# Layer 0 of a two-layer graph network: the heads' product placed two node blocks later, the joined words in two copies, and the source scores of 13 row blocks transposed together

## The chip, the cores and the metric

The kernel runs on one core of one Trainium2 chip. The metric is the time of one execution on the device, in microseconds. The core has five engines with queues of their own: PE (matrix products, with PEld for its weight loads), DVE (vector), ACT (scalar), POOL and SP. The last two mostly issue transfers here. The transfers run on 16 DMA engines.

## The reference

There are 3327 nodes with 1024 features each. Layer 0 normalises the rows, quantises them, multiplies them by a quantised weight and by the weighted adjacency matrix, and adds the result to the input. Layer 1 normalises again, projects to 8 attention heads of 64, attends over the neighbours, and sends the result through four dense layers.

```python
# layer 0
h = jnp.maximum(_layernorm(x, axis=-1), 0.0)
x = x + _L0_gnn_ref(h, adj, ...)        # relu(xq @ wq), quantised; then adj @ support_q
# layer 1
h = jnp.maximum(_layernorm(x, axis=-1), 0.0)
...
Wh = jnp.einsum('nf,hfd->hnd', x, W)
e_src = jnp.einsum('hnd,hd->hn', Wh, a1)
e_dst = jnp.einsum('hnd,hd->hn', Wh, a2)
e = jax.nn.leaky_relu(e_src[:, :, None] + e_dst[:, None, :], ALPHA)
e = jnp.where(adj[None] > 0, e, NEG)
att = jax.nn.softmax(e, axis=-1)
h = jnp.einsum('hnm,hmd->hnd', att, Wh)
...
```

## The kernel before

Nodes are cut into T = 26 blocks of 128. A first stage quantises and makes the support `s_int` (26 tiles of 128 x 1024 that stay on the chip). It ends at about 125 us in the profile.

The second stage is the one that is changed. Its loop runs over 26 row blocks t of the output. For each of them the PE sums over 26 node blocks j the product of the adjacency (split into `hi` and `lo`, two fp32r parts) with `s_int[j]`: four products of 512 columns per j (two parts, two column halves), 104 per row block (L680). The j are taken in four groups, `PARTS`, of 7, 6, 7 and 6. `adjacency` loads a group on SP (`at`, L170, three buffers), casts it on ACT (`hi`, L174, two buffers), subtracts on DVE (`lo`, L178, two buffers), and writes the mask (`mk`, L179). It is called one group ahead.

After the 104 products of block t, ACT takes the sum out of PSUM (`y`, L695), DVE scales it (L696), adds the input (`xt`, L697, two buffers, loaded on SP at L128), POOL issues the store of that sum (`x1_d`, printed `x_d` in the profile, L698), and DVE makes the statistics of the layer norm and the normalised rows (L143 to L150). Then the rows are transposed for the heads (`transposed_by_dma`): ACT splits the 32-bit words into two 16-bit halves (`yh`, L587), SP issues a transposing DMA (`yht`, L589), and ACT joins the halves again (`ht`, L591). The last block is transposed by the PE instead.

`heads(t)` projects the rows: eight products of 512 columns (`whm`, L614; each shows twice in the profile, x16 for a block), a copy with the row's scale on ACT (`wht`, L620), two weighted sums on DVE (`src` and `dst`, L627 and L628), exponentials on ACT, a small PE transposition of `src` from 128 x 8 to 8 x 128 (`sp`, L633), its copy (`srct`, L635) and its store (`src_d`, L638, on POOL). Then come the features `ft`, `fw`, `dw` and their stores (`feat_d` L658, `dsum_d` L662, on POOL). The heads of block t run one row block later, in front of the last group of j of block t + 1:

```python
                    if js is PARTS[-1] and before is not None:
                        heads(*before)
                    for q, j in enumerate(js):
```

The order of instructions on each engine is fixed when the kernel is built, by a planner that follows estimated times, except for the instructions that `keep_in_program_order` pins. Each engine and each issuing queue works in that order.

The third stage, layer 1's attention, reads the stored features and source scores back (`f_even`, `f_odd`, `dw`, `srow`, on SP), makes the selection `sel` on DVE (L984) and multiplies on the PE (L993, L786). Its first products run between the last blocks of the second stage. The fourth stage is the dense layers.

Of the kernel before, what the change touches and what calls it, by code (L numbers as in the profile page):

```python
# [8 lines left out]
F32 = mybir.dt.float32  # L9
# [11 lines left out]
P = 128  # L21
N = 3327
T = (N + P - 1) // P
# [3 lines left out]
KF = F // P  # L27
FC = F // 512
NH = 8
# [13 lines left out]

SUBS = [range(0, 7), range(7, 13), range(13, 20), range(20, 26)]
PARTS = SUBS
GT = 2


# [12 lines left out]
def two_layer_kernel(  # L61
# [23 lines left out]
    nc = tc.nc  # L85

    const = ctx.enter_context(tc.tile_pool(name="const", bufs=1))
    dram = ctx.enter_context(tc.tile_pool(name="dram", bufs=1, space=DRAM))
    small = ctx.enter_context(tc.tile_pool(name="small", bufs=4))

    ident = const.tile([P, P], F32, name="ident")
    make_identity(nc, ident)
    ident_b = const.tile([P, P], BF16, name="ident_b")
    nc.vector.tensor_copy(ident_b, ident)
    ones = const.tile([P, P], F32, name="ones")
    nc.gpsimd.memset(ones, 1.0)
    nth = const.tile([P, P], F32, name="nth")
    nc.gpsimd.memset(nth, 1.0 / P)


    x1_d = dram.tile([NP, F], F32, name="x1_d")
# [3 lines left out]
    src_d = [dram.tile([NH, len(sub) * P], F32, name=f"src_d{i}") for i, sub in enumerate(SUBS)]  # L105
    enc_d = dram.tile([2, NP, EMB], U16, name="enc_d")

    const.tile([P, 32], F32, name="gap")
    ndst = const.tile([P, T, NH], F32, name="ndst")
    ratio = const.tile([P, T, NH], F32, name="ratio")  # L110


# [40 lines left out]
    def halves_of_words(words):  # L153

        return words.bitcast(U16).rearrange("p (n two) -> p two n", two=2)
# [7 lines left out]
    with tc.tile_pool(name="at", bufs=2, reuse_waits="tile") as atp:  # L163
# [35 lines left out]
        with tc.tile_pool(name="s1", bufs=2, reuse_waits="tile") as s1, tc.tile_pool(  # L199
            name="s1_mm", bufs=3, space=PSUM, reuse_waits="tile"  # L200
        ) as mm_ps, tc.tile_pool(name="s1_tp", bufs=2, space=PSUM, reuse_waits="tile") as tp_ps:
            w_int = s1.tile([P, KF, F], BF16, name="w_int", bufs=1)
            w_stats = s1.tile([P, 2 + 4 * (KF - 2), 3], F32, name="w_stats", bufs=1)

# [338 lines left out]
            for t in range(8, T):  # L543
                if t == T - 2:
                    part = next(columns)
# [26 lines left out]
        with tc.tile_pool(name="wh", bufs=1, reuse_waits="tile") as whp, tc.tile_pool(  # L572
            name="s2", bufs=2, reuse_waits="tile"
        ) as s2, tc.tile_pool(name="mm", bufs=2, space=PSUM, reuse_waits="tile") as mm_ps, tc.tile_pool(
            name="s2_wh", bufs=2, space=PSUM, reuse_waits="tile"
# [8 lines left out]
            def transposed_by_dma(y):  # L584

                yh = s2.tile([P, 2, F], U16, name="yh", bufs=1)
                nc.scalar.copy(yh, halves_of_words(y))  # L587
                yht = s2.tile([P, 2 * KF, P], U16, name="yht", bufs=1)
                nc.sync.dma_start_transpose(yht, yh.rearrange("p two f -> p (two f)"))  # L589
                ht = s2.tile([P, KF, P], F32, name="ht", bufs=1)  # L590
                nc.scalar.copy(  # L591
                    halves_of_words(ht.rearrange("p k i -> p (k i)")),
                    yht.rearrange("p (two k) i -> p two (k i)", two=2),
                )
                return ht

            def transposed_by_tensor(y):
# [9 lines left out]
            def heads(t, ht, r):  # L607
                if t == T - 1:
                    whm, sp = (last_ps.tile([P, EMB], F32, tag="last", name=n) for n in ("whm", "sp"))
                else:  # L610
                    whm = wh_ps.tile([P, EMB], F32, name="whm")
                    sp = sp_ps.tile([P, EMB], F32, name="sp")
                for k in range(KF):
                    ins = nc.tensor.matmul(  # L614
                        whm, ht[:, k, :], whead[:, k, :], start=(k == 0), stop=(k == KF - 1)
                    )
                    if k == 0 and t < T - 1:
                        tc.keep_in_program_order(ins)
                wht = s2.tile([P, EMB], F32, name="wht", bufs=1)
                ins = nc.scalar.activation(wht, whm, AF.Copy, scale=r)  # L620
                if t < T - 1:
                    tc.keep_in_program_order(ins)
                src = small.tile([P, NH], F32, name="src")
                dst = small.tile([P, NH], F32, name="dst")
                for a_t, e in ((a1_t, src), (a2_t, dst)):
                    prod = s2.tile([P, EMB], F32, name="prod", bufs=1)
                    nc.vector.tensor_tensor(prod, wht, a_t, ALU.mult)  # L627
                    nc.vector.tensor_reduce(  # L628
                        e, prod.rearrange("p (h d) -> p h d", d=HD), AX.X, ALU.add
                    )  # L630
                nc.vector.tensor_scalar(ndst[:, t], dst, -1.0, None, ALU.mult)
                nc.scalar.activation(ratio[:, t], src, AF.Exp, scale=1.0 - SLOPE)
                nc.tensor.transpose(sp[:NH, :P], src, ident)  # L633
                srct = s2.tile([NH, P], F32, name="srct")
                nc.scalar.copy(srct, sp[:NH, :P])  # L635
                for sub, d in zip(SUBS, src_d):
                    if t in sub:
                        nc.gpsimd.dma_start(d[:, (t - sub[0]) * P : (t - sub[0] + 1) * P], srct)  # L638

                ft = s2.tile([P, NH, 2, HC], F32, name="ft", bufs=1)  # L640
                wh3 = wht.rearrange("p (h d) -> p h d", d=HD)
                for q, slope in enumerate((1.0, SLOPE)):
                    nc.scalar.activation(ft[:, :, q, HD], dst, AF.Exp, scale=slope)
                    nc.vector.tensor_tensor(
                        ft[:, :, q, :HD], wh3, ft[:, :, q, HD:].to_broadcast([P, NH, HD]), ALU.mult
                    )
                fw = s2.tile([P, NH, 2, 2 * HC], F32R, name="fw", bufs=1)
                f2 = ft.rearrange("p h q c -> p h (q c)")
                nc.scalar.copy(fw[:, :, 0], f2)
                nc.vector.tensor_tensor(fw[:, :, 1], f2, fw[:, :, 0].bitcast(F32), ALU.subtract)  # L650

                dw = s2.tile([P, NPAIR, 2, 2, HC], F32R, name="dw", bufs=1)
                for q in range(2):
                    nc.scalar.copy(
                        dw[:, :, q],
                        fw[:, :, q, HC:].bitcast(F32).rearrange("p (g e) c -> p g e c", e=2),
                    )
                nc.gpsimd.dma_start(  # L658
                    feat_d[t].rearrange("h p c -> p h c"),
                    fw.bitcast(F32).rearrange("p h q c -> p h (q c)"),  # L660
                )
                nc.gpsimd.dma_start(  # L662
                    dsum_d[t].rearrange("g p c -> p g c"),
                    dw.bitcast(F32).rearrange("p g q e c -> p g (q e c)"),
                )

            before = None
            for t in range(T):
                xt = s2.tile([P, F], F32, name="xt2")
                load_rows(xt, x, t)  # L670
                mm = mm_ps.tile([P, F], F32, tag="mm", name="mm2")
                for js in PARTS:
                    hi, lo = part
                    part = next(columns, None)
                    if js is PARTS[-1] and before is not None:
                        heads(*before)
                    for q, j in enumerate(js):
                        for which in (hi, lo):
                            for c in range(FC):
                                nc.tensor.matmul(  # L680
                                    mm[:, c * 512 : (c + 1) * 512],
                                    which[:, q, :],
                                    s_int[j][:, c * 512 : (c + 1) * 512],
                                    start=(j == 0 and which is hi),
                                    stop=(j == T - 1 and which is lo),
                                )
                if t == 0:
                    for dst, ap in (
                        (whead, w_heads.rearrange("(k p) e -> p k e", p=P)),
                        (a1_t, a1.partition_broadcast(P)),  # L690
                        (a2_t, a2.partition_broadcast(P)),
                    ):
                        tc.keep_in_program_order(nc.sync.dma_start(dst, ap))
                y = s2.tile([P, F], F32, name="y", bufs=1)
                nc.scalar.activation(y, mm, AF.Copy, scale=r_asf)  # L695
                nc.vector.tensor_scalar(y, y, asf_t, sup_delta, ALU.mult, ALU.mult)  # L696
                nc.vector.tensor_tensor(xt, xt, y, ALU.add)  # L697
                nc.gpsimd.dma_start(x1_d[t * P : (t + 1) * P, :], xt)  # L698
                ln, r = normalised(y, xt)
                before = t, (transposed_by_tensor if t == T - 1 else transposed_by_dma)(y), r  # L700
# [419 lines left out]
```

## Time and profile before

| what | value |
|---|---|
| median of 3 runs | 2240.1 us (2240.02 to 2240.91) |
| profiled execution | 2241.67 us, span 2239.9 us |
| granted PE clock | 0.998 |
| layer 0's second stage | from about 125 to 936 us of the span |
| PE wait for `ht` | 7.0 us, 7 times, longest 1.4 |
| small transposition L633 | 26 times, 7.1 us busy, 273 ns each |
| copy `ht`, L591 | 25 times, 2.51 us each |
| transposing DMA `yht` | 25 times, 5.5 us from issue to landing (median) |
| store of `src_d` | 26 times, 4 KB, 1.6 us from issue to landing (median) |

The profile is one execution. Its times are in us from the first instruction. A line of the timeline gives start, duration, engine, line of the kernel, operation, what is written and what is read, the shapes, how many instructions were merged, and in brackets the idle time of the engine before it and what ended it. A group's line has busy time, mean ns of one and idle time. The PE's ends are modelled, so differences between starts are the safer measure there.

### The profile page before, as it was taken

To read this page: it belongs to the slowest core of one execution; us is meant where nothing else is said; L and a number is where in the kernel's file an instruction comes from. 1 tells how busy PE (TensorE), PEld (TensorE's weight loads), DVE (VectorE), ACT (ScalarE), POOL (GpSimd) and SP (SyncE) were. 2 spreads that over 40 slices of the span, in tenths; PEclk is the share of its full clock that TensorE was granted. 3 is DMA by queue.
4 is the path that set the end of the run, shared out by engine and by line. 5 is a ranking of instruction groups with operands and counts; after the bars stand their busy time and mean duration, and the time that the engine had idled before them with its cause. 6 is when DMAs were issued, how large, how long until landed. Compare 5 with 4: busy or idle time off the path is not lost.

```text
span 2239.9 us, 31268 instructions
## 1 busy us (share of the span) xinstructions
PE 2190.0 (98%) x12470; PEld 1747.2 (78%) x12480; DVE 1536.8 (69%) x1996; ACT 1114.9 (50%) x1685; POOL 180.4 (8%) x269
## 2 busy tenths in 40 slices
PE   5999999999999999899999999999999999999998
PEld 2477777766677777699999999999999999744444
DVE  8745555554455545588999999999999999822211
ACT  6734444444454444357566556565555655531120
POOL 2301101110111101000000000000000000000000
PEclk9999999999999999999999999999999999999999
DMA  6665566555665556934242341654242432383311
GB/s 216 161 196 158 157 182 183 170 168 146 183 181 171 162 158 189 310 128 148 83 139 88 93 131 33 225 175 151 86 148 83 138 89 77 100 208 104 113 56 56
DMA packets 241203, 321.68 MB, mean 144 GB/s; under 512 B 104021, under 2 KB 184869, under 8 KB 241057
## 3 DMA queue, kind: packets, MB, share of 16 engines
q1 hardware_dynamic: 220504, 246.50, 36.8%
q0 software_dynamic: 20544, 73.18, 10.4%
q8 instruction: 98, 1.61, 0.3%
q14 instruction: 49, 0.39, 0.1%
q10 hardware_dynamic: 8, 0.00, 0.0%
HBM read 209.25 MB, written 86.79 MB: 132 GB/s over the span
## 4 chain that ended last, share of the span: by engine, by line
PE 53%; ACT 1%; DVE 0%; DMA 0%; issue 0%; DVEq 0%
PE acc L993 27%; PE mps L786 13%; PE o L1064 8%; PE h_ps L1027 4%; ACT enct L1049 0%; PE h_ps L949 0%; DMA weights<-in_w1t 0%; ACT h L1034 0%; DVE sel L984 0%; DVE nodes L1060 0%; ACT su L830 0%; DVE su L827 0%; DVE yo L1074 0%; ACT rest L957 0%; DVEq L1117 0%
## 5 line engine op out<-in xcount | busy, mean ns | idle before, releaser
L984 DVE SCALAR_TENSOR_TENSOR sel<-srow,ndst,mask 128x896 fp32r<-128x896 f32 (+1 forms) x832 | 864.8, 1081 | 52.3 <-PE acc L993 47.2
L786 PE MATMUL mps<-dw,mf 128*128 128x260 f32 x2704 | 452.4, 283 | 0.1
L680 PE MATMUL mm<-s_int,hi 128*128 128x512 f32 x1352 | 427.2, 397 | 0.0
L680 PE MATMUL mm<-s_int,lo 128*128 128x512 f32 x1352 | 419.1, 391 | 0.0
L993 PE MATMUL acc<-f_even,sel 128*128 128x260 f32 x2704 | 399.6, 285 | 6.7 <-issue 5.0
L993 PE MATMUL acc<-f_odd,sel 128*128 128x260 f32 x2704 | 393.8, 286 | 1.0 <-ACT xs L1008 1.0
L785 ACT CAST mf<-mask 128x1664 fp32r<-128x1664 uint8 x208 | 331.4, 1594 | 113.0 <-PE mps L786 94.9
L786 PEld LDWEIGHTS mps<-dw,mf 128*128 128x128 f32 x2704 | 377.2, 188 | 0.5 <-ACT part L790 0.3
L993 PEld LDWEIGHTS acc<-f_even,sel 128*128 128x128 f32 x2704 | 356.8, 189 | 11.7 <-issue 5.9
L993 PEld LDWEIGHTS acc<-f_odd,sel 128*128 128x128 f32 x2704 | 352.5, 188 | 8.4 <-issue 3.4
L680 PEld LDWEIGHTS mm<-s_int,hi 128*128 128x128 f32 x1352 | 253.9, 188 | 63.6 <-issue 12.0
L680 PEld LDWEIGHTS mm<-s_int,lo 128*128 128x128 f32 x1352 | 252.0, 188 | 51.4
L179 DVE TENSOR_SCALAR mk<-at 128x896 uint8<-128x896 f32 (+1 forms) x104 | 62.0, 598 | 227.1 <-DMA at<-in_adj_t 226.8
L614 PE MATMUL whm<-whead,ht 128*128 128x512 f32 x416 | 184.4, 596 | 7.2 <-ACT ht L591 7.0
L1064 PE MATMUL o<-weights,h 128*128 128x512 f32 x416 | 179.9, 592 | 0.0
L1064 PEld LDWEIGHTS o<-weights,h 128*128 128x128 f32 x416 | 79.0, 190 | 99.3 <-issue 98.3
L614 PEld LDWEIGHTS whm<-whead,ht 128*128 128x128 f32 x416 | 77.6, 190 | 101.0 <-issue 87.1
L174 ACT CAST hi<-at 128x896 fp32r<-128x896 f32 x104 | 92.4, 889 | 125.6 <-PE mm L680 85.2
L790 ACT COPY part<-mps 128x260 f32<-128x260 f32 x104 | 39.3, 378 | 193.8 <-PE mps L786 193.8
L178 DVE TENSOR_TENSOR lo<-at,hi 128x896 fp32r<-128x896 f32 x104 | 106.0, 1020 | 42.8 <-ACT hi L174 42.6
L855 POOL DMA_DIRECT2D enc_d<-eh x64 | 57.5, 903 | 935.6 <-ACT eh L853 876.0
L1034 ACT ACTIVATE h<-h_ps,rest 128x512 f32<-128x512 f32 (+1 forms) x54 | 35.1, 653 | 195.0 <-PE h_ps L1027 195.0
(162 smaller groups left out, 1676.9 us busy)
## 6 DMA issues: line engine op xcount, KB each, us to landing
feat_d<-fw POOLq DMA_DIRECT2D x26, 1040.0 KB, 5.4
f_even<-feat_d SPq DMA_DIRECT2D x7, 3380.0 KB, 13.3
f_odd<-feat_d SPq DMA_DIRECT2D x7, 3380.0 KB, 13.2
at<-in_adj_t SPq DMA_DIRECT2D x52, 448.0 KB, 3.8
at<-in_adj_t SPq DMA_DIRECT2D x52, 384.0 KB, 3.2
mask<-mask_d SPq DMA_DIRECT2D x39, 416.0 KB, 6.5
dw<-dsum_d SPq DMA_DIRECT2D x16, 910.0 KB, 8.9
dsum_d<-dw POOLq DMA_DIRECT2D x26, 520.0 KB, 6.4
```

Source lines behind the costliest of these rows:

```text
L174: ins = nc.scalar.copy(hi, at)
L178: nc.vector.tensor_tensor(lo, at, hi.bitcast(F32), ALU.subtract)
L179: ins = nc.vector.tensor_scalar(mk[:, r], at, 0.0, None, ALU.is_gt)
L614: ins = nc.tensor.matmul(whm, ht[:, k, :], whead[:, k, :], start=(k == 0), stop=(k == KF - 1))
L680: nc.tensor.matmul(mm[:, c * 512 : (c + 1) * 512], which[:, q, :], s_int[j][:, c * 512 : (c + 1) * 512], start=(j == 0 and which is hi), s ...
L785: nc.scalar.copy(mf, mask[:, j : j + TH, :])
L786: nc.tensor.matmul(ps, mf[:, j % TH, :], dw[:, j, :], start=(j == 0), stop=(j == T - 1))
L855: nc.gpsimd.dma_start(enc_d[q, sub[0] * P : (sub[-1] + 1) * P, h * HD : (h + 1) * HD].rearrange("(b p) d -> p b d", p=P), eh[:, q].rearran ...
L984: nc.vector.scalar_tensor_tensor(sel[:, :nb], srow[:, :nb], ndst[:, j, h : h + 1], mask[:, :, j, :], ALU.is_gt, ALU.mult,)
L993: nc.tensor.matmul(accs[b], sel[:, b, :], f[:, j, :], start=(j == 0), stop=(j == T - 1))
L1027: nc.tensor.matmul(ps[:, :cols], wt[:, k, m * P : (m + 1) * P], xt[:, k, :cols], start=(k == 0), stop=(k == k_n - 1),)
L1064: nc.tensor.matmul(ps[:, c * 512 : (c + 1) * 512], h3[:, k, q * P : (q + 1) * P], w4[:, k, c * 512 : (c + 1) * 512], start=(k == 0), stop= ...
```

## The change

In the second stage `heads` is called after two node blocks of the last group instead of ahead of it, except in the last row block, where its place stays. The joining copy `ht` becomes two copies, one for each half of the features. The source scores of all blocks stay in one tile `srcs`; they are transposed, copied and stored in three batches: blocks 0 to 12 after block 12, blocks 13 to 24 after block 24, and block 25 by itself. The stores of a batch are still one per block. To make room, two constants of the first stage (`ones`, `nth`) move into a pool of that stage, and a filler tile grows.

```diff
+BATCHES = {12: 0, T - 2: 13, T - 1: T - 1}
...
-    const.tile([P, 32], F32, name="gap")
+    const.tile([P, 112], F32, name="gap")
     ndst = const.tile([P, T, NH], F32, name="ndst")
+    srcs = const.tile([P, T, NH], F32, name="srcs")
...
-                nc.scalar.copy(
-                    halves_of_words(ht.rearrange("p k i -> p (k i)")),
-                    yht.rearrange("p (two k) i -> p two (k i)", two=2),
-                )
+                halves = yht.rearrange("p (two k) i -> p two k i", two=2)
+                for k in range(0, KF, KF // 2):
+                    part = slice(k, k + KF // 2)
+                    nc.scalar.copy(
+                        halves_of_words(ht[:, part].rearrange("p k i -> p (k i)")),
+                        halves[:, :, part].rearrange("p two k i -> p two (k i)"),
+                    )
                 return ht
...
-                src = small.tile([P, NH], F32, name="src")
+                src = srcs[:, t]
...
-                nc.tensor.transpose(sp[:NH, :P], src, ident)
-                srct = s2.tile([NH, P], F32, name="srct")
-                nc.scalar.copy(srct, sp[:NH, :P])
-                for sub, d in zip(SUBS, src_d):
-                    if t in sub:
-                        nc.gpsimd.dma_start(d[:, (t - sub[0]) * P : (t - sub[0] + 1) * P], srct)
+                if t in BATCHES:
+                    first = BATCHES[t]
+                    n = (t + 1 - first) * NH
+                    nc.tensor.transpose(
+                        sp[:n, :P], srcs[:, first : t + 1].rearrange("p t h -> p (t h)"), ident
+                    )
+                    srct = s2.tile([P, P], F32, name="srct")
+                    nc.scalar.copy(srct[:n], sp[:n, :P])
+                    for u in range(first, t + 1):
+                        d, sub = next((d, sub) for d, sub in zip(src_d, SUBS) if u in sub)
+                        nc.gpsimd.dma_start(
+                            d[:, (u - sub[0]) * P : (u - sub[0] + 1) * P],
+                            srct[(u - first) * NH : (u - first + 1) * NH],
+                        )
...
-                    if js is PARTS[-1] and before is not None:
-                        heads(*before)
                     for q, j in enumerate(js):
+                        if js is PARTS[-1] and q == (2 if t < T - 1 else 0) and before is not None:
+                            heads(*before)
                         for which in (hi, lo):
```

More of the change, by code (lines that the diff above doesn't have):

```diff
@@ L94, in two_layer_kernel @@
     nc.vector.tensor_copy(ident_b, ident)
[L95 to L98, printed above, removed]
     x1_d = dram.tile([NP, F], F32, name="x1_d")
@@ L201, in two_layer_kernel @@
         ) as mm_ps, tc.tile_pool(name="s1_tp", bufs=2, space=PSUM, reuse_waits="tile") as tp_ps:
+            ones = s1.tile([P, P], F32, name="ones", bufs=1)
+            nc.gpsimd.memset(ones, 1.0)
+            nth = s1.tile([P, P], F32, name="nth", bufs=1)
+            nc.gpsimd.memset(nth, 1.0 / P)
             w_int = s1.tile([P, KF, F], BF16, name="w_int", bufs=1)
```

## The prediction

> **What bounds the kernel now.** I read the page's busy times first, then the waits of the PE, then the timeline of one row block of layer 0 on each engine.
>
> ```profile
> PE 2190.0 (98%) x12470; PEld 1747.2 (78%) x12480; DVE 1536.8 (69%) x1996; ACT 1114.9 (50%) x1685; POOL 180.4 (8%) x269
> ...
> L614 PE MATMUL whm<-whead,ht 128*128 128x512 f32 x416 | 184.4, 596 | 7.2 <-ACT ht L591 7.0
> ```
>
> The PE is busy for 98% of the span, in layer 0 as in layer 1, and behind it there is no other long chain: what the PE saves in layer 0 comes off the end, as long as nothing else becomes late. The second line names one wait inside layer 0: the heads' product waits for the joined words `ht`. The waits of the PE give 7.0 us in 7 places. Idle time is counted there from a modelled end, so I count starts instead. This is block 15's piece on the PE, columns start, duration, line:
>
> ```profile
> 606.09 0.62 PE L680 MATMUL mm<-s_int,hi 128*128 128x512 f32 x2
> 606.54 0.61 PE L680 MATMUL mm<-s_int,lo 128*128 128x512 f32 x2
> 608.57 7.13 PE L614 MATMUL whm<-whead,ht 128*128 128x512 f32 x16 [1.42 <-ACT ht L591]
> ...
> 617.39 0.63 PE L680 MATMUL mm<-s_int,hi 128*128 128x512 f32 x2
> 617.93 0.27 PE L633 MATMUL sp<-ident,src 128*8 128x128 f32 x1
> 617.96 0.71 PE L680 MATMUL mm<-s_int,lo 128*128 128x512 f32 x2
> 618.51 0.62 PE L680 MATMUL mm<-s_int,hi 128*128 128x512 f32 x2
> ```
>
> Products of layer 0 start every 0.227 us (two in 0.45). The second of the pair at 606.54 starts at 606.77, so L614 was due at 607.00 and began at 608.57: 1.58 us lost, not 1.42. Going through all 25 blocks that way, 12 are late, by 0.04, 0.15, 0.20, 0.21, 0.23, 0.97, 0.98, 1.01, 1.09, 1.17, 1.33 and 1.58 us: **8.9 us**. In 15 blocks the second product of L614 also follows the first after 0.53 us in place of 0.43, because its weights were not loaded ahead: 15 x 0.105 = **1.6 us**. In all 10.5 us of PE time hang on `ht`. The last lines show what the small transposition costs: from 617.39 to 618.51 four products and the transposition take 1.12 us, where the four alone need 0.91: **0.21 us** per block.
>
> Why `ht` is late shows on the other engines in the block before:
>
> ```profile
> 590.36 1.11 ACT L695 ACTIVATE y<-mm,r_asf 128x1024 f32<-128x1024 f32 x1
> ...
> 596.84 1.90 ACT L587 COPY yh<-y 128x2048 uint16<-128x2048 uint16 x1 [0.94 <-DVE y L146]
> ...
> 606.04 2.48 ACT L591 COPY ht<-yht 128x2048 uint16<-128x2048 uint16 x1 [4.80 <-DMA yht<-yh]
> ```
>
> ```profile
> 597.90 0.33 SPq L170 DMA_DIRECT2D at<-in_adj_t  x1
> 598.77 3.66 SPq L589 DMA_TRANSPOSE yht<-yh  x1
> 602.48 0.58 SPq L128 DMA_DIRECT2D xt<-in_x  x1
> ```
>
> The block's last product ended at 589.02. `y` began 1.34 us later, because ACT was still at `fw`; then come the layer norm on DVE, `yh`, the transposing DMA (7.3 us here, 5.3 to 5.5 in blocks without a wait) and 2.48 us of `ht`. The whole chain has nearly no slack: without a wait `ht` starts 13.8 to 14.0 us after `y`, and 14.3 already costs 0.2 us.
>
> [...]
>
> **The change, part by part**, against the profiled execution (2241.67 us, span 2239.9; the median of the runs is 2240.1, 1.6 lower; I take differences from the one to the other).
>
> *Transpositions at once.* L633, its copy L635 and its wait disappear in 23 of 26 blocks; blocks 12, 24 and 25 keep one (104, 96 and 8 columns). 23 x 0.21 = 4.9 us of PE; the two wide ones load more weights (83 ns for 8 columns, 190 for 128), at most 0.1 us each: **-4.8 us**, with nothing to hide it. DVE's work is the same. ACT saves 0.26 us per block, off the path.
>
> *The small stores.* 26 of them either way, 4 KB each, 0.54 us on POOL and 1.0 to 1.6 us to land. Now 13 in a row after block 12 (7.0 us), 12 after block 24 (6.5 us). Queued behind them: x1, `feat_d` and `dsum_d`. After block 12 that delays them by 1 to 2 us; the next writer of `fw` comes 30 us later: nothing. After block 24 `feat_d` is issued about 2.2 us later (at 935.0 for 932.80), lands near 945 for 942.7, and SP, which waits for it in front of `f_even` of block 24, is as late; that load landed at 953.5 and is first used at 975: 20 us of cover, nothing. If that cover were gone, its 2.2 us would show.
>
> *Heads two blocks later.* Eight products earlier in the queue: L614 falls due 8 x 0.227 = 1.82 us later, except at the last iteration (heads of block 24), where the place is kept. But the heads' own work now ends nearer to the block's end, and the built order of each engine shifts: ACT runs `y` ahead of `hi` and `fw`, DVE runs `lo`, `xt`, `fw` ahead of the layer norm, and another `lo` ahead of its last step. With the durations of block 14: `wht` at 585.16, `ft` done on ACT at 589.08, last product at 588.81, so `y` starts 0.27 us after it (1.34 before). DVE: `y` from 590.35 for 0.81, `lo` 0.96, `xt` 1.23, `fw` 1.25, statistics 1.28, mask 0.6, aggregate 0.2, `lo` 1.08, `y` 0.73: `yh` begins at about 598.5 and ends at 600.4, 11.6 us after the block's last product, 9.7 before. The transposition is **1.87 us later** for a product that is due **1.82 us later**: this part alone gives nothing. It also puts the third group of `lo` (done near 604.6) ahead of its products at 606.6 without the heads in between: 2.0 us of cover where there were 11.
>
> *Joined words in two halves.* The first four products need only the first copy: [...] 1.34 us, 1.14 earlier. The second comes 1.3 us after the first and is needed 4 x 0.86 us after it. So **1.1 us** of margin per block: of the waits above, 0.07 and 0.48 us remain, and three times 0.1. In the last iteration the chain is 1.0 us later with no later due time: 1.33 + 1.03 - 1.14 = 1.2, and a third mask load now stands ahead of the transposition: 1.2 to 2.2, I take 1.6. In all 2.5 of 10.5 us remain: **-8.0 us**.
>
> *SP's order*, not seen in steady state before: the load of `xt` two blocks on now stands ahead of the transposition, and waits for that block's x1 store. x1 stands now ahead of `feat_d` and `dsum_d` on POOL: issued near 593.4, with 2.9 us to land where nothing was ahead of it (first block), so free at 596.3, or at 600.1 with the 6.7 us it takes behind the two big stores; the transposition is ready at 600.4. [...] Bounds: nothing (in the first block `xt` was issued at 159.19 and the transposition at 161.16, and it took 5.4 us as elsewhere), up to 3 us per block (4.1 us of `xt` load fully ahead). I take nothing, by the first block; a gain is excluded but for a few tenths, as what is moved ahead was behind.
>
> The constants moved to a pool of stage 1 change no instruction there: nothing. The 5.0 us of PE idle between the layers stay: `y`, `xt` and `sel` on DVE keep their order.
>
> **Sum:** -4.8 - 8.0 = -12.8: 2228.9 for a profiled execution, **2227.3 us** for the median.
>
> **Rivals.**
> - *The waits stay.* The transposition gets 1.0 to 1.3 us slower by the `xt` load ahead of it, and the halves are used up. For it: its 5.3 to 7.8 us in the trace vary with other traffic. Then only -4.8 to -6: 2234 to 2235.3.
> - *Slower: SP becomes the bound.* With d us more per transposition, the wait is d - 1.3 in 22 blocks (0.2 of old slack and 1.1 of new); from d = 1.9 on, 22 x 0.6 = 13 us eat the whole gain. At d = 2.5, 26 us: 2253. [...] Against it: the first block, and that the x1 store is no longer behind 1.5 MB.
> - *The third `lo` is late.* It waits behind a mask step for an adjacency load that landed up to 1.2 us late in some blocks; its cover is 2.0. If 1 us is lost in the eight bad blocks, the gain is 4.8: 2235.
>
> **How the numbers follow.** A measurement of this kernel tells about 0.2% (4.5 us, below 2235.6) from no change. The sum's case has 0.63, its own range 2224 (no wait left, 15.3 us, and a little off the uneven starts after each transposition) to 2231. The waits that stay and the late `lo` have 0.25, of which 0.14 falls under 2235.6 and the rest within 0.2%. A slower kernel has 0.10, and 0.02 fall within 0.2% from nearly cancelling terms. So faster 0.77, same 0.13, slower 0.10. The range goes from 2223 to 2239: it leaves out 0.05 below and 0.13 above.
>
> **What would show it.** Right: L633 three times; `mm` starts 0.227 apart where it stood; `ht` as 50 copies near 1.34 us; the PE's wait for `ht` under 2 us and mostly in the last iteration; `y` 0.3 us after the last product. Wrong: an SP transposition that takes over 6.5 us in most blocks, SP waiting for the x1 store ahead of it, or a PE wait for `lo` at L680; a span above 2236 would mean that the gain was eaten there.

## The result, and the profile after

The changed kernel takes **2245.3 us** (median of 17 runs, 2240.19 to 2248.24) where the kernel before took 2240.91 us (median of 17, 2238.72 to 2242.59). The ratio is **1.0016, 95% interval 1.0010 to 1.0023**: 0.16% slower, which is inside what I had called no change, far from the 2227.3 us that I forecast and outside the range of 2223 to 2239. The profiled execution took 2246.18 us, its span is 2244.4 us (before 2241.67 and 2239.9).

The page's busy times and two of its costliest groups (count | busy, mean ns of one | idle before them and what ended it):

```profile
PE 2190.3 (98%) x12447; PEld 1748.7 (78%) x12457; DVE 1525.3 (68%) x1996; ACT 1106.7 (49%) x1687; POOL 181.2 (8%) x269
...
L619 PE MATMUL whm<-whead,ht 128*128 128x512 f32 x416 | 186.9, 603 | 11.7 <-ACT ht L596 11.3
...
L596 ACT COPY ht<-yht 128x1024 uint16<-128x1024 uint16 x50 | 63.5, 1334 | 139.8 <-DMA yht<-yh 139.8
```

The two copies are there, 50 of 1.33 us, and still the heads' product waits longer for `ht` than before: 11.3 us where it was 7.0. The waits of the PE give it 16 times (us in total, times, longest), and show that the rival of the late `lo` was nearly nothing:

```profile
PE whm L619 <- ACT ht L596: 11.3, 16, 2.0
...
PE mm L693 <- DVE lo L176: 0.8, 1, 0.8
```

I take block 19 as an example, since its transposition took about the median time. This is the timeline of the PE, ACT, SP and POOL from its `y` to its product (start, duration, engine, line):

```profile
743.45 1.10 ACT L708 ACTIVATE y<-mm,r_asf 128x1024 f32<-128x1024 f32 x1
...
752.17 1.90 ACT L589 COPY yh<-y 128x2048 uint16<-128x2048 uint16 x1 [2.00 <-DVE y L144]
...
762.08 2.54 ACT L596 COPY ht<-yht 128x1024 uint16<-128x1024 uint16 x2 [5.77 <-DMA yht<-yh]
```

```profile
752.16 0.99 SPq L126 DMA_DIRECT2D xt<-in_x  x1
754.09 5.97 SPq L591 DMA_TRANSPOSE yht<-yh  x1
```

```profile
747.80 0.55 POOL L711 DMA_DIRECT2D x_d<-xt  x1 [7.60 <-DVE xt L710]
748.95 0.91 POOL L671 DMA_DIRECT2D feat_d<-fw  x1 [0.60 <-DVE fw L663]
749.85 0.85 POOL L675 DMA_DIRECT2D dsum_d<-dw  x1
```

```profile
762.13 0.62 PE L693 MATMUL mm<-s_int,hi 128*128 128x512 f32 x2
762.59 0.61 PE L693 MATMUL mm<-s_int,lo 128*128 128x512 f32 x2
763.47 0.70 PE L619 MATMUL whm<-whead,ht 128*128 128x512 f32 x1 [0.27 <-ACT ht L596]
```

Three things are to be seen. SP issues the `xt` load 1.93 us ahead of the transposition. The issue of the transposition itself lasts 5.97 us, where it was 3.66 in the block shown of before, and `ht` starts 7.99 us after it. On the PE the product was due at 762.59 + 0.45 = 763.04 and began at 763.47, 0.43 late. On POOL, `feat_d` and `dsum_d` are issued 5.50 and 6.40 us after `y`; before they were issued 1.7 and 2.6 us after it (medians), and had landed by 7.1 and 8.9.

Read that way for blocks 1 to 22, the whole chain from `y` to the heads' product can be set against its due time (medians in us):

| step | before | after | difference |
|---|---|---|---|
| `y` starts, to the issue of the transposition | 8.41 | 10.76 | +2.35 |
| issue, to the start of `ht` | 5.60 | 8.04 | **+2.44** |
| start of `ht`, to the first product when it waits | 2.54 | 1.39 | -1.15 |
| the chain | 16.55 | 20.19 | +3.64 |
| `y` starts, to the time when the product is due | 16.64 | 19.59 | +2.95 |
| slack | +0.09 | **-0.60** | |

A slack of -0.60 is a PE that is late in a typical block (the median lateness is 0.64). Summed over the trace, the products are late by 12.9 us in blocks 0 to 23 and by 2.2 in the last iteration, and the second product adds 2.4 in 23 blocks (0.105 each) and 1.7 more after the last wait (see the end): 19.3 us, and 0.9 for a late `lo`. Before it was 10.5. The small transpositions gave their 4.8 back. So +9.7 - 4.8 = +4.9 us is the account of the second stage, which is 5.5 us longer by its own ends (807.3 for 801.9); its start was 1.9 earlier and the rest 1.0 later, so that the span is 4.5 longer.

### The profile page after: what moved, and what is told of

Same layout as the page of the kernel before. It is cut to its first block, busy times and chain, and to the rows that moved or that the text cites. A ratio compares the mean times of both kernels' runs of the same rounds, so it can differ in the third digit from the quotient of the medians.

```text
span 2244.4 us, 31226 instructions
## 1 busy us (share of the span) xinstructions
PE 2190.3 (98%) x12447; PEld 1748.7 (78%) x12457; DVE 1525.3 (68%) x1996; ACT 1106.7 (49%) x1687; POOL 181.2 (8%) x269
## 4 chain that ended last, share of the span: by engine, by line
PE 53%; ACT 1%; DVE 0%; DMA 0%; issue 0%; SPq 0%; DVEq 0%
PE acc L1006 27%; PE mps L799 13%; PE o L1077 8%; PE h_ps L1040 4%; ACT enct L1062 0%; PE h_ps L962 0%; DMA weights<-in_w1t 0%; DVE sel L997 0%; ACT h L1047 0%; DVE nodes L1073 0%; SPq L947 0%; ACT su L843 0%; DVE su L840 0%; DVE yo L1087 0%; ACT rest L970 0%
## 5 line engine op out<-in xcount | busy, mean ns | idle before, releaser
L619 PE MATMUL whm<-whead,ht 128*128 128x512 f32 x416 | 186.9, 603 | 11.7 <-ACT ht L596 11.3
L619 PEld LDWEIGHTS whm<-whead,ht 128*128 128x128 f32 x416 | 77.6, 191 | 109.6 <-issue 88.2
L596 ACT COPY ht<-yht 128x1024 uint16<-128x1024 uint16 x50 | 63.5, 1334 | 139.8 <-DMA yht<-yh 139.8
L1087 DVE TENSOR_TENSOR yo<-o,nodes 128x1024 f32<-128x1024 f32 (+1 forms) x27 | 31.8, 1182 | 136.5 <-PE o L1077 136.4
```

The source lines that it names most:

```text
L596: nc.scalar.copy(halves_of_words(ht[:, part].rearrange("p k i -> p (k i)")), halves[:, :, part].rearrange("p two k i -> p two (k i)"),)
L619: ins = nc.tensor.matmul(whm, ht[:, k, :], whead[:, k, :], start=(k == 0), stop=(k == KF - 1))
```

## The experiments

The question is where the forecast gain of 12.8 us went, and the 4.4 us that the kernel lost besides. Theory A: the transposition became slower (8.04 us to `ht` for 5.60) because SP now issues the `xt` load ahead of it, with two forms. A1: its place in SP's queue, behind the `xt` load, is what costs. A2: 512 KB more under way at that time is what costs, whichever queue brings them. The rivals: the stores of `feat_d` and `dsum_d`, which now come at the same time, do it (theory B in the expectations); or the later place of the heads itself, with a chain too long whatever the transfers do (C), or the batches (C') or the copies cost what they should have saved. The eight runs below share runs of the kernel before (2240.13 us for the first four, 2240.34 for the others).

**The heads two blocks later, alone** (`e4_later`, on the kernel before):

```diff
-                    if js is PARTS[-1] and before is not None:
-                        heads(*before)
                     for q, j in enumerate(js):
+                        if js is PARTS[-1] and q == (2 if t < T - 1 else 0) and before is not None:
+                            heads(*before)
```

> The kernel before with the one edit of the heads' products two node blocks later; 26 small transpositions and one copy of ht as before. By the prediction's step this part alone gives nothing: 2238 to 2243. Theory A or B, where this edit alone brings SP's new order and the later stores: every block waits about 1.15 us longer than in the changed kernel (no half copy) and has the small transposition, so 25 to 35 us more than the changed kernel: 2268 to 2282, with the transposition at 7.5 to 9 us.

Measured: 2276.76 us (2273.76 to 2280.44, 4 runs), ratio 1.0165 (1.0151 to 1.0179). Its PE waits and two lines of its DMA issues (count, KB, median us to landing):

```profile
PE whm L614 <- ACT ht L591: 33.9, 23, 2.7
```

```profile
xt<-in_x SPq DMA_DIRECT2D x25, 512.0 KB, 7.9
...
yht<-yh SPq DMA_TRANSPOSE x25, 7.7
```

The one edit that I had priced at nothing costs 36.6 us by itself, and brings the slow transposition (7.92 us to `ht`) and the new orders of SP, POOL, ACT and DVE with it. Its slack by the table's steps is 19.70 - 10.68 - 7.92 - 2.54 = -1.44; the median lateness is 1.47. The forecast "gives nothing" fails here by itself, and the time is in the range for theories A and B.

**Batches and copies, the heads where they were** (`e3_batch_halves`, on the kernel after):

```diff
-                        if js is PARTS[-1] and q == (2 if t < T - 1 else 0) and before is not None:
-                            heads(*before)
+                    if js is PARTS[-1] and before is not None:
+                        heads(*before)
```

> The changed kernel with the heads' products back in front of the last group; batches and two copies kept. The planner then keeps the kernel before's order on SP and DVE. Theory A and B alike, since neither the xt load nor the stores move: transposition 5.3 to 5.5 us in most blocks, the PE's wait for ht about 1 us in all, 23 small transpositions less: 8 to 15 us faster than the kernel before, 2226 to 2233. Theory C': the batches of 13 and 12 stores cost something of their own after blocks 12 and 24: less than 5 us faster.

Measured: **2227.22 us** (2225.14 to 2228.32, 5 runs), ratio 0.9942 (0.9929 to 0.9954). SP's order is that of the kernel before, the transposition takes 5.6 us, and the PE waits three times:

```profile
PE whm L619 <- ACT ht L596: 2.5, 3, 1.1
```

So the later place of the heads makes this kernel 18.1 us slower (2245.3 - 2227.2), and the other two parts give 12.9 together. The two medians were not taken beside the same runs of the kernel before; each against its own, it is 4.4 + 12.9 = 17.3.

**The changed kernel, with the `xt` load behind the transposition** (`e1_xt_behind`): only SP's order changes, DVE, ACT and POOL keep theirs.

```diff
-                nc.sync.dma_start_transpose(yht, yh.rearrange("p two f -> p (two f)"))
+                turns.append(nc.sync.dma_start_transpose(yht, yh.rearrange("p two f -> p (two f)")))
...
-                load_rows(xt, x, t)
+                with tc.issue_after(turns[t - 2].ins) if t >= 2 else nullcontext():
+                    load_rows(xt, x, t)
```

> The changed kernel with one edge more: the load of xt two blocks on is queued on SP behind the transposing DMA, as in the kernel before; every other engine keeps the changed kernel's order. Theory A [...]: issue to landing returns to 5.3 to 6.3 us, the PE's wait for ht falls from 11.3 us to under 3, and the time falls by 10 to 16 us against the changed kernel, to 2229 to 2235. Theory B (the feat and dsum stores, which now start 5.5 and 6.4 us after y in place of 1.7 and 2.6, overlap the transposition and slow it): still over 7 us to landing, and the time stays within 3 us of the changed kernel's. Theory C (the chain ahead of the transposition is too long, whatever the transfers do): the time stays too, with the transposition at 5.4.

Measured: 2229.59 us (2227.78 to 2232.37, 5 runs), ratio 0.9951 (0.9938 to 0.9965). Its PE waits, its DMA issues, and SP in block 19:

```profile
PE whm L619 <- ACT ht L596: 3.5, 2, 1.9
```

```profile
xt<-in_x SPq DMA_DIRECT2D x25, 512.0 KB, 4.1
...
yht<-yh SPq DMA_TRANSPOSE x25, 6.1
```

```profile
744.81 4.12 SPq L591 DMA_TRANSPOSE yht<-yh  x1
749.04 0.53 SPq L126 DMA_DIRECT2D xt<-in_x  x1
```

One transfer changes its place in the queue, and 15.7 us come back (4.4 + 10.5 = 14.9, each against its own runs of the kernel before). The transposition is issued 10.75 us after `y`, as in the kernel after, and takes 6.19 to `ht` for 8.04: the load ahead of it costs 1.85 us. The slack is 19.56 - 10.75 - 6.19 - 1.39 = +1.23. This is the run that shows theory A: the stores come as late as in the changed kernel and the chain ahead of the transposition is as long, so neither B nor C can be the bulk of it.

**The kernel before, with the `xt` load ahead of the transposition** (`e2_before_xt_ahead`): the opposite test. The load of block t + 2 is written ahead of the transposition and pinned there.

```diff
-                nc.sync.dma_start_transpose(yht, yh.rearrange("p two f -> p (two f)"))
+                tc.keep_in_program_order(nc.sync.dma_start_transpose(yht, yh.rearrange("p two f -> p (two f)")))
...
+                if t + 2 < T:
+                    load_xt(t + 2)
                 before = t, (transposed_by_tensor if t == T - 1 else transposed_by_dma)(y), r
```

> The kernel before with one edge changed: the load of xt two blocks on is queued on SP ahead of the transposing DMA. It also has to wait there for the x1 store, which in this kernel lands about 10.3 us after y, so the transposition's issue moves from 8.4 to about 10.9 us after y: some 2.5 us in 23 blocks, 50 to 60 us, in any theory. Theory A: on top of it the transposition takes 7.5 us or more from issue to landing in place of 5.3 to 5.5, so 2320 to 2350 us. Theory B: the transposition takes 5.3 to 5.8 us, since no store has moved, and the time is 2290 to 2305.

Measured: 2332.04 us (2329.4 and 2334.68), ratio 1.0411 (1.0392 to 1.0430). In this kernel x1 is stored behind `feat_d` and `dsum_d`, and the load, which waits for that store, holds SP. SP's waits between 180 and 900 us, and the PE's between 180 and 935:

```profile
SPq L128 <- DMA x_d<-xt: 50.3, 21, 4.0
```

```profile
PE whm L614 <- ACT ht L591: 61.2, 22, 4.8
```

The transposition is issued 2.1 us later per block, and then takes 6.44 for 5.60 to `ht`: 2.9 us late in a typical block (the median lateness is 2.9). The test is therefore a mixture of two mechanisms, and the slower transposition is the smaller part of it. The expectation set 7.5 us or more for theory A and 5.3 to 5.8 for B: the 6.44 is neither. What it does give is a transposition with no store beside it: at its issue, 10.5 us after `y`, all three have landed (medians 7.1, 9.0 and 10.1), and with the load it is 0.84 longer than in the kernel before. The pair isn't clean, since in the kernel before x1's store is still under way for the first 2.0 us of the transposition, and since the load is issued 0.4 us ahead here and 1.9 in the changed kernel.

**The `xt` load on POOL's queue** (`e5_xt_pool`, on the kernel after; it tells A1 from A2):

```diff
-            nc.sync.dma_start(dst[r], ap[t * P + r.start : t * P + r.stop, :])
+            engine.dma_start(dst[r], ap[t * P + r.start : t * P + r.stop, :])
...
-                load_rows(xt, x, t)
+                load_rows(xt, x, t, nc.gpsimd if t >= 2 else nc.sync)
```

> The changed kernel with the load of xt (from block 2 on) issued by POOL behind the feat and dsum stores, in place of SP. It still starts 8 to 9 us after y, ahead of the transposing DMA[...]. Theory A1 [...]: issue to landing of the transposition 6.0 to 6.6 us, the PE's wait for ht under 4 us, 2228 to 2233 us. Theory A2 (it is enough that 512 KB more are under way then, whichever queue issued them): 7.3 to 8.5 us, 2240 to 2248 us.

Measured: 2249.51 us (2248.98 to 2255.41, 5 runs), ratio 1.0048 (1.0035 to 1.0060).

```profile
PE whm L619 <- ACT ht L596: 22.1, 23, 4.4
```

```profile
xt<-in_x POOLq DMA_DIRECT2D x23, 512.0 KB, 8.2
...
yht<-yh SPq DMA_TRANSPOSE x25, 8.3
```

The load is issued about 1.7 us ahead of the transposition, from another queue, and the transposition takes 8.3 us to its landing all the same (8.3 in the kernel after too), inside A2's range; the time is 1.5 us above it. A1 falls: behind the load in SP's queue or not, the transposition takes as long. In the prediction I had weighed only the order within SP's queue.

**The batches alone** (`e6_batch`: the diff's `BATCHES`, `srcs`, `srct` and the constants' pool, on the kernel before):

```diff
-                src = small.tile([P, NH], F32, name="src")
+                src = srcs[:, t]
...
-                nc.tensor.transpose(sp[:NH, :P], src, ident)
+                if t in BATCHES:
...
+                    nc.tensor.transpose(
+                        sp[:n, :P], srcs[:, first : t + 1].rearrange("p t h -> p (t h)"), ident
+                    )
```

> The kernel before with the batches alone: one copy of ht, heads' products in front of the last group. By the prediction's step 23 transpositions at 0.21 us come off the PE and nothing else changes: 4 to 6 us faster than the kernel before, 2234 to 2237. The rival that the bursts of 13 and 12 stores cost something: within 2 us of the kernel before, with a longer wait for ht in blocks 12 and 13 or at the change of layers.

Measured: 2238.29 us (2235.75 to 2241.74, 13 runs), ratio 0.9991 (0.9983 to 0.9999).

```profile
PE whm L616 <- ACT ht L593: 9.5, 8, 2.2
```

Only 2.1 us of the 4.8 come out (0.2 to 3.8 by the interval). It isn't that the removed work had been cover: from `y` to the due time it is 16.64 us here as before, since the small transposition stood ahead of `y`. But the late starts of the heads' product sum to 11.3 us in its profile for 9.0 before, and 4.8 - 2.3 = 2.5 is about what was measured. Blocks move both ways: 10, 12 and 13 are 1.5, 2.3 and 2.3 us late here (0.2, 1.0 and 1.1 before), while 14 is on time (1.6 late before). The transpositions of blocks 12 and 13 take 8.1 and 8.0 us (6.4 and 6.8 before). They are slow in `e3_batch_halves` (7.9, 8.1) and `e1_xt_behind` (7.5, 9.4) too, less so in `e7_halves` below (7.1, 6.6), which has no batches. Block 12's transposition runs ahead of the heads of block 12, so ahead of the first batch's stores: these can't be its cause, and what is stays open. In block 13 they may have a part, as the expectation's rival had it: the 13 small stores stand on POOL ahead of `feat_d`, `dsum_d` and x1, and 0.75 MB of POOL's stores are under way during the transposition for 0.41 before.

The transpositions between 400 and 600 us are slower than the others: in blocks 1 to 23 the medians to `ht` are 6.5 and 5.4 us in the kernel before, 8.4 and 7.8 in the kernel after. Something else goes with that: during most of them one packet of 16 KB runs on the queue that the page prints as `q8 instruction`. The median with such a packet, and without, is 6.5 and 5.5 us in the kernel before, 8.4 and 7.8 in the kernel after, 7.4 and 6.1 in `e1_xt_behind`. No run tested whether it is the cause.

**The two copies alone** (`e7_halves`, on the kernel before):

```diff
-                nc.scalar.copy(
...
+                for k in range(0, KF, KF // 2):
+                    part = slice(k, k + KF // 2)
+                    nc.scalar.copy(
...
```

> The kernel before with the two copies of ht alone. By the prediction's step the first four products can start 1.14 us earlier, so of the 10.5 us of waits in the kernel before 1 to 3 remain: 7 to 10 us faster, 2230 to 2234. If the second copy were late for the fifth product, or the weights of the first were still not loaded ahead: 3 to 6 us faster.

Measured: 2232.68 us (2231.13 to 2233.42, 5 runs), ratio 0.9963 (0.9949 to 0.9976): 7.7 us faster. No wait for `ht` is listed, and the late starts sum to 0.5 us.

**The repaired kernel, with the heads of block 23 at the old place** (`e8_behind_t24`: `e1_xt_behind` and one number):

```diff
-                        if js is PARTS[-1] and q == (2 if t < T - 1 else 0) and before is not None:
+                        if js is PARTS[-1] and q == (2 if t < T - 2 else 0) and before is not None:
```

> The changed kernel with the xt load behind the transposition, and with the heads' old place kept in the last two row blocks instead of the last one, so that block 24's chain starts as early as in the kernel before. Where the 2.1 us wait (and 1.7 us of slow products behind it) for ht in the last iteration comes from the later start of that chain: the wait falls under 1.2 us and the time is 2 to 4 us below the version with the edge alone, 2225 to 2228. If the wait only moves one block earlier: within 1.5 us of that version, 2228 to 2231.

Measured: 2227.44 us (2226.39 to 2228.30, 5 runs), ratio 0.9942 (0.9929 to 0.9954). The last wait falls from 2.07 to 0.41 us. It is as fast as `e3_batch_halves`, and both beat the kernel before by 13 us: once the waits are gone, the later place gives nothing.

## Why the prediction was wrong, point by point

**SP's order was the step that failed.** I wrote: "*I take nothing, by the first block*", with bounds of 0 and 3 us per block, the upper one an estimate from the 4.1 us that the load takes. The transposition became 2.44 us longer. This table puts the medians of seven kernels together, in us from issue to `ht`, by what was under way beside it:

| at the issue of the transposition | `feat_d`, `dsum_d` landed, or 0.5 us from it | both under way |
|---|---|---|
| no `xt` load ahead | 5.6 (before, `e3_batch_halves`) | 6.2 (`e1_xt_behind`) |
| `xt` load ahead | 6.4 (`e2_before_xt_ahead`, 0.4 us ahead) | 8.0 (after), 7.9 (`e4_later`), 8.3 on POOL's queue (`e5_xt_pool`) |

Read so, each alone costs 0.6 to 0.8 us, the two together 2.4. What the right column shows is sound: with the stores where they are, the load ahead costs 1.85 us. That the two cost more together than their sum is not shown as well, because the left column differs in other ways too. In the upper left the end of x1's store is under way (a median of 0.39 MB on POOL's queue between issue and `ht`, 0.51 MB in the kernels after and `e1_xt_behind`), in the lower left nothing of POOL's. No run keeps the load 1.9 us ahead and puts the stores back early.

The first block, on which I leaned, belongs to the lower left: no heads precede it, so its `feat_d` and `dsum_d` stores do not exist yet, and it took 5.6 us in the changed kernel too. Over the traces, with the load 1.35 to 2.1 us ahead, it took 5.4 to 5.6 us, and with the load behind (`e1_xt_behind`, `e8_behind_t24`) 5.2 and 5.1. I had its order of SP right and missed that its neighbours on POOL were absent. Two blocks of the changed kernel have the load behind the transposition. Block 23 took 5.1 us and was not late (in `e1_xt_behind` it is quick too, 4.8 for a median of 6.2, so the order is not all of it). Block 13 took 8.4 all the same: x1's store had stood behind the 13 small stores, was issued 7.75 us after `y` for 4.35, and 1.0 MB of POOL's stores were under way.

**POOL's order** I had used for one thing only, that x1 lands earlier. It did: 7.9 us after `y`, well ahead of the load, and after the first block SP waited for it once, for 1.3 us. But the same reordering moves `feat_d` and `dsum_d` (1.5 MB) from landing at 7.1 and 8.9 us to 11.6 and 14.2, the last part of them (a median of 0.51 MB) on top of the transposition. The prediction counted these stores in the path of x1 and not in that of the transposition.

**Heads later "gives nothing":** the two terms were 1.87 us later for a product due 1.82 later. Measured from the block's last product, which `y` now follows 1.1 us sooner, the transposition is issued 2.35 - 1.12 = 1.2 us later, and the due time moved by 1.8 as supposed. That is 0.6 us per block better than predicted, and it was eaten: alone, the edit costs 36.6 us, because of the orders that it brings.

**The halves** had the right size. The 1.34 us of a copy was an estimate; measured are 1.33, and the two last 2.54 us together in block 19, where the one copy took 2.51. Of margin 1.14 us were predicted, 1.15 measured, and 7.7 us by themselves for the 8.0 that I summed. In the changed kernel the margin went into the slower transposition.

**The transpositions at once**: the 4.8 us of PE work went, but alone they gave 2.1. The sum lacked that late starts elsewhere would grow at the same time (2.3 us, with the largest rises in blocks 10, 12 and 13), for which no cause was shown. With the halves, whose margin takes most of that up, they give what was summed: 12.9 us for both against 12.8.

**The rivals.** "The waits stay" named the cause, the load ahead of the transposition, with too small a size: 1.0 to 1.3 us for 2.44. "SP becomes the bound" allowed for the size, with the wrong name: SP began nothing late, the transfer took longer. It asked for a d over 1.9 us to eat the gain, and gave d - 1.3 as the wait. Measured d is 2.44, and with the 0.6 above the wait is 2.44 - 1.3 - 0.6 = 0.5 us; the table's slack shows 0.6. I had given it 0.10. The predicted 2.5 us of remaining waits became 20.2 with the second products and `lo`; of the last iteration's 1.6, 2.2 was measured, and 1.7 behind it.

**Right** were the fall of the small transpositions, the copies at 1.33 us, `y` 0.2 us after the last product (0.3 forecast), the small stores in a row without effect on the waits of layer 1 (in block 13 they held x1's store back by 3.4 us, where I had put 1 to 2 us and no cost), and the idle stretch at the change of layers (5.0 us in both). The mark that I set for being wrong, a transposition over 6.5 us in most blocks, is what happened. Two readings of the kernel before were slightly off, and nothing hangs on them: the twelve late starts sum to 9.0 us, not 8.9, and without a wait the transposition takes 5.1 to 5.8 us, not 5.3 to 5.5.

## What to carry to other kernels

Moving one step of this program, whose engines are ordered by a planner, moved the transfers too: `feat_d` was issued 5.5 us after `y` for 1.7, and the `xt` load ahead of the transposition. Before giving a transfer on a tight chain its old duration, list what is under way on all queues at its new issue time, and take as a model only a place where the same transfers are under way. Whether a chain is tight is read from one table, its steps against its due time, and every new duration has to be carried through that table. Here two of the three parts without the third make the better kernel (2227.2 us), and so does one load put back behind one transposition (2229.6).

## What the runs showed of the hardware that was not expected

The issue of the transposing DMA on SP was itself longer with other traffic under way: 3.6 us (median) in the kernel before, 4.2 with the two stores (`e1_xt_behind`), 5.7 with stores and load (after), 6.0 with the load on POOL's queue (`e5_xt_pool`). What stood behind it on SP moved with it: in block 19 of the kernel after the next adjacency load is issued at 760.78, 0.72 us after the end of that issue. Most of the lost time passed before the transposition moved anything. Its 2048 packets of 256 bytes begin 2.4 us after the issue in the kernel before and 4.4 in the kernel after and in `e5_xt_pool`; from the first to the end of the last it is 2.7 us before and 2.8 after (medians of blocks 1 to 22). In `e2_before_xt_ahead` they begin after 2.5 us, though it takes 6.44 to `ht`, another pattern. Why the first packet came so late, even with the load on another queue, is not shown.

After the last wait of the kernel after, the PE's products run at half pace for a while: from 920.64 to 924.02 us they start 0.85 us apart, where it is 0.43 otherwise. The last iteration's 16 records of L619 take 8.83 us, those of another block 7.13:

```profile
577.66 7.13 PE L619 MATMUL whm<-whead,ht 128*128 128x512 f32 x16 [0.90 <-ACT ht L596]
...
919.65 8.83 PE L619 MATMUL whm<-whead,ht 128*128 128x512 f32 x16 [2.03 <-ACT ht L596]
```

That is 1.7 us on top of a wait of 2.03. In `e4_later` it came after late starts of 1.98, 2.47, 2.50 and 2.91 us, but not after others of 2.00 to 2.44, so the length of the wait alone doesn't tell it. The clock records of the traces show what goes with it. In the kernels before and after, every change of the granted clock lies a multiple of 3.413 us from the others. Cut there, two stretches of the kernel after, at its last wait (after the length comes the PE's busy time with its count, then those of PEld, DVE, ACT and POOL, and the granted clock):

```profile
917.16:920.57 3.41, 1.38 (x5) 0.52 (x4) 0.00 (x0) 2.30 (x2) 0.00 (x0) 1.00 1.02 293
920.57:923.98 3.41, 3.41 (x5) 1.35 (x4) 0.00 (x0) 0.22 (x1) 0.00 (x0) 0.50 1.02 362
```

Two of `e4_later`, at the start that was 2.44 us late:

```profile
555.42:558.83 3.41, 2.54 (x12) 1.77 (x10) 0.03 (x1) 1.10 (x1) 0.00 (x0) 1.00 0.98 244
558.83:562.25 3.42, 2.00 (x5) 1.05 (x6) 1.72 (x2) 2.16 (x2) 0.00 (x0) 1.00 0.02 6
```

The half clock lasts one stretch here and follows a stretch in which the PE was busy for 1.38 of 3.41 us, 0.40 of it. In `e4_later` the wait fell across two stretches, in which the PE was busy for 2.54 of 3.41 and 2.00 of 3.42 us, and nothing happened. Between 130 and 930 us of the ten traces (busy times with modelled ends), 19 stretches at full clock had the PE busy for 0.43 of their length or less, and half clock followed all of them; 2285 had 0.48 or more, and it followed none; of the 7 between, it followed 4. These are counts of this case; what sets the clock is not shown. The granted clock of the whole profiled run went from 0.998 to 0.996 (after), 0.993 (`e4_later`) and 0.986 (`e2_before_xt_ahead`).
